# Cross-attention with layer norm: a tile's scores with 128 rows as weights in place of 64

## The chip, the cores and the metric

The kernel runs on one NeuronCore of a Trainium2 chip. The metric is device time in microseconds (us) of one execution. Three runs of the kernel before took 506.99 to 508.13 us, median 507.49.

The engines are called as in the profile: PE is TensorE, and its matmuls; PEld is TensorE's loading of weights, the operand that stays in the array while the other one streams past; DVE is VectorE, ACT is ScalarE, POOL is GpSimd, SP issues transfers (DMA).

## The reference

Four sequences of 2048 rows of 512 numbers attend to 77 context rows each, with 16 heads of 32 numbers. Then comes an output projection, the residual and a layer norm. All is fp32.

```python
qs = (q @ wq).reshape(Bq, Lq, H, HD).transpose(0, 2, 1, 3)       # H = 16, HD = 32
ks_ = (k @ wk).reshape(Bq, Lk, H, HD).transpose(0, 2, 1, 3)      # Lk = 77
vs = (v @ wv).reshape(Bq, Lk, H, HD).transpose(0, 2, 1, 3)
scores = jnp.einsum('bhqd,bhkd->bhqk', qs, ks_) / jnp.sqrt(jnp.float32(HD))
scores = jnp.where(mask[:, None, :, :], -jnp.inf, scores)
attn_w = jax.nn.softmax(scores, axis=-1)
attn = jnp.einsum('bhqk,bhkd->bhqd', attn_w, vs)
attn = attn.transpose(0, 2, 1, 3).reshape(Bq, Lq, H * HD)
out = attn @ wo + q
mu = jnp.mean(out, axis=-1, keepdims=True)
var = jnp.mean((out - mu) ** 2, axis=-1, keepdims=True)
return (out - mu) / jnp.sqrt(var + EPS) * gamma + beta
```

## The kernel before

The 8192 rows are 64 tiles of 128 rows. Keys and values are made once, at the start. Then each tile goes through these steps, each of them a word in a long table, `ORDER`, that is written out by hand and read from left to right; every engine works off its own instructions in that order.

- `Q`: the queries of four tiles, kept transposed: 512 rows of x stream past the weights `wq`. A product of high precision is made of three fp32r matmuls, of rounded parts (`q_rows`, line 275). VectorE copies the result to `q` (line 289).
- `S`: the scores of a tile (line 405), the step that is changed.
- `T`: VectorE adds the mask to the scores and takes each row's maximum (line 422); it reads them from the bank that TensorE wrote.
- `e`, `r`, `n`: exponentials by ScalarE (line 437), reciprocals by VectorE, the product by GpSimd (line 452).
- `t`, `P`: VectorE transposes 32x32 blocks (line 473), and transfers regroup them (line 484).
- `V`: the weights times the values, of two tiles at once (line 498), split into two parts for the next step by ScalarE and VectorE.
- `O`: the output projection (line 554), again three matmuls for each product. Residual, moments, scale, gain, shift and store follow on the other engines.

So TensorE's queue is a sequence of visits: 12 matmuls for a fourth of a `Q`, 12 for an `O`, a visit for the values, a visit for the scores. Between words, 62 visits make the scores of 64 tiles: 60 of one tile, and two, early in the run, of two tiles.

In `scores`, the queries of the tile are the weights and the keys stream. A head has 32 numbers, so it uses a band of 32 of the array's 128 rows, and the four heads j of a group lie on the four bands. `SR` is how many rows of the tile one matmul takes as weights, which are as many columns of the array. With 64, the two halves r0 = 0 and 64 of a tile use the left and the right half of the columns, and their results go to the lower and the upper 64 partitions of the bank. A group has so eight matmuls on eight pieces of the array, and a tile has four groups. Each fp32 matmul of the program runs as two pairs of a weight load and a matmul.

```python
SR = 64                                                        # line 42
...
for g in range(NG):                                            # line 401, four groups
    for r0 in range(0, P, SR):
        for j in range(GH):                                    # four heads of a group
            q = slice(HD * j, HD * (j + 1))
            mm = nc.tensor.matmul(
                sc[j][r0 : r0 + SR, g * NK : (g + 1) * NK],    # line 406, out
                qs[q, g, rs.start + r0 : rs.start + r0 + SR],  # weights: 32 x SR
                kct[q, g, t // TPB, keys_of(j)],               # streams: 32 x 77
                start=True,
                stop=True,
            )
```

Of the kernel before, what the change touches and what calls it, by code (L numbers as in the profile page):

```python
# [38 lines left out]
MASKED = -3.38e38  # L39
EPS = 1.0e-5  # L40
WARM = 9
SR = 64
NPB = 3
KSCALE = 1.0 / HD**0.5
LAST = 56
# [129 lines left out]
def xattn_layernorm(  # L175
# [74 lines left out]
    def keys_of(h):  # L250
        return slice(TAIL_K, NK2) if h % 2 == 0 else slice(0, NK)
# [145 lines left out]
    def scores(t):  # L397
# [3 lines left out]
        for g in range(NG):  # L401
            for r0 in range(0, P, SR):
                for j in range(GH):
                    q = slice(HD * j, HD * (j + 1))
                    mm = nc.tensor.matmul(  # L405
                        sc[j][r0 : r0 + SR, g * NK : (g + 1) * NK],
                        qs[q, g, rs.start + r0 : rs.start + r0 + SR],
                        kct[q, g, t // TPB, keys_of(j)],
# [392 lines left out]
```

## Time and profile before

| what | us |
|---|---|
| median of three runs | 507.49 |
| span of the profiled execution | 506.2 |
| PE busy | 498.8 |
| ACT busy | 473.9 |
| DVE busy | 460.5 |
| POOL busy | 421.3 |
| scores' matmuls (line 405), busy | 61.2 |
| scores' weight loads (line 405), busy | 51.4 |

The profile is of one execution. The page gives its span, from the first to the last instruction, and no time of its own beyond that. Busy times count a moment once however many instructions of a kind run in it, so many small matmuls side by side show a busy time far below the sum of their lengths. In a row of the timeline the first number is the start, the second the length of the whole group of equal instructions that follow each other, and "x64" their count; a row is cut to what falls in the stretch that was asked for. A shape such as 32*64 behind a matmul is the piece of the array in rows and columns.

### The profile page before, as it was taken

The numbers are of one execution on the slowest core, as the hardware profiler recorded it, in microseconds if no ns is written. First come the engines' busy times: TensorE is split into PE (matmuls) and PEld (weight loads), VectorE is DVE, ScalarE is ACT, GpSimd is POOL, SyncE is SP. The second block draws the span as 40 slices with busy tenths as digits, with TensorE's granted clock in tenths as the row PEclk, the third lists the DMA queues.
The fourth block names the chain that finished last, engine by engine and source line by source line (L and its number), as shares of the span: only waits on it lengthen the run. The fifth ranks groups of instructions, "written<-read, shape, count | busy, mean of one in ns | idle before, by whom it ended". The sixth has DMA issues, their size and how long they took to land.

```text
span 506.2 us, 20312 instructions
## 1 busy us (share of the span) xinstructions
PE 498.8 (99%) x6831; PEld 383.1 (76%) x6831; DVE 460.5 (91%) x2539; ACT 473.9 (94%) x2248; POOL 421.3 (83%) x387
## 2 busy tenths in 40 slices
PE   9999999999999999999999999999999999999995
PEld 6987778777777777777777777777777777877773
DVE  5799988999899999898898898998999999899997
ACT  6699999999999999999999999999999998999851
POOL 2666464789886798989989887999998999999896
PEclk9999999999999999999999999999999999999999
DMA  8957577889886796859887778877888769888746
GB/s 306 396 197 175 135 212 183 221 210 217 247 242 178 177 248 199 249 165 253 243 216 204 200 207 240 230 201 193 248 232 225 207 177 293 247 199 222 183 150 232
DMA packets 58782, 110.86 MB, mean 219 GB/s; under 512 B 9462, under 2 KB 11278, under 8 KB 58678
## 3 DMA queue, kind: packets, MB, share of 16 engines
q1 hardware_dynamic: 54502, 101.30, 71.1%
q0 software_dynamic: 2496, 5.77, 4.0%
q10 hardware_dynamic: 1680, 2.49, 2.0%
q8 instruction: 54, 0.88, 0.8%
q14 instruction: 50, 0.41, 0.3%
HBM read 41.79 MB, written 16.78 MB: 116 GB/s over the span
## 4 chain that ended last, share of the span: by engine, by line
PE 98%; DMA 1%; DVE 1%; ACT 0%; issue 0%; DVEq 0%
PE po L554 36%; PE pq L275 35%; PE pa L498 11%; PE sc L405 11%; PE pv L326 2%; PE pk L299 1%; PE pq L685 1%; DMA stage_a<-kin 1%; PE pa L513 0%; DVE xtl L637 0%; PE po L543 0%; DVE st L606 0%; DVE po L634 0%; ACT woh L672 0%; DVE mvt L608 0%
## 5 line engine op out<-in xcount | busy, mean ns | idle before, releaser
L437 ACT ACTIVATE pbuf<-pbuf,nm 128x77 f32<-128x77 f32 x1024 | 353.0, 358 | 5.2 <-DVE nm L422 3.6
L437 ACT ACTIVATION_READ_ACCUMULATOR pbuf<-pbuf,nm 128x1 f32 x1024 | 203.2, 198 | 0.0
L422 DVE CUSTOM_DVE_ANT_0 pbuf<-sc,mb 128x77 f32<-128x77 f32 x1024 | 169.7, 231 | 7.4 <-PE sc L405 5.8
L452 POOL TENSOR_TENSOR pbuf<-pbuf,ri 128x1232 f32<-128x1232 f32 x63 | 142.2, 2258 | 36.7 <-DVE ri L447 25.4
L554 PE MATMUL po<-woh,AH 128*128 128x512 f32 x256 | 103.5, 404 | 0.0
L473 DVE STREAM_TRANSPOSE B<-pbuf 128x1280 f32<-128x1280 f32 x64 | 96.1, 1502 | 5.8 <-POOL pbuf L452 2.4
L275 PE MATMUL pq<-xth,wqh 128*128 128x512 f32 (+1 forms) x256 | 100.8, 394 | 0.2
L554 PE MATMUL po<-wol,AH 128*128 128x512 f32 x256 | 99.9, 390 | 0.0
L554 PE MATMUL po<-woh,AL 128*128 128x512 f32 x256 | 99.8, 390 | 0.0
L275 PE MATMUL pq<-xth,wql 128*128 128x512 f32 (+1 forms) x256 | 98.1, 383 | 0.0
L275 PE MATMUL pq<-xtl,wqh 128*128 128x512 f32 (+1 forms) x256 | 98.1, 383 | 0.0
L422 DVE DVE_READ_ACCUMULATOR2_ANT nm<- 128x1 f32 x1024 | 84.4, 82 | 0.0
L598 POOL TENSOR_TENSOR o<-o,bet 128x512 f32<-128x512 f32 x56 | 72.1, 1291 | 1.8
L595 POOL TENSOR_TENSOR o<-o,gam 128x512 f32<-128x512 f32 x56 | 72.2, 1293 | 0.1
L269 POOL TENSOR_TENSOR xtl<-xtf,xth 128x1024 fp32r<-128x1024 f32 x28 | 67.2, 2404 | 3.9 <-ACT xth L265 3.2
L405 PEld LDWEIGHTS sc<-kct,q 32*64 32x64 f32 x4096 | 51.4, 130 | 22.6 <-issue 12.2
L405 PE MATMUL sc<-kct,q 32*64 32x77 f32 x4096 | 61.2, 238 | 0.0
L498 PE MATMUL pa<-PT,vsb 96*32 96x256 f32 x992 | 59.7, 382 | 0.0
L554 PEld LDWEIGHTS po<-woh,AH 128*128 128x128 f32 x256 | 48.0, 188 | 14.3 <-issue 2.5
L275 PEld LDWEIGHTS pq<-xth,wqh 128*128 128x128 f32 x256 | 48.1, 188 | 13.7 <-DVE nm L422 1.2
L554 PEld LDWEIGHTS po<-woh,AL 128*128 128x128 f32 x256 | 48.1, 188 | 10.5 <-DVE AL L531 0.2
L275 PEld LDWEIGHTS pq<-xth,wql 128*128 128x128 f32 x256 | 48.1, 188 | 9.7
(108 smaller groups left out, 638.6 us busy)
## 6 DMA issues: line engine op xcount, KB each, us to landing
PT<-B SPq DMA_DIRECT2D x330, 128.0 KB
xtf<-xT SPq DMA_DIRECT2D x28, 512.0 KB
o<-x SPq DMA_DIRECT2D x56, 256.0 KB
out<-o SPq DMA_DIRECT2D x56, 256.0 KB
PT<-B POOLq DMA_DIRECT2D x25, 128.0 KB, 4.0
PT<-B ACTq DMA_DIRECT2D x17, 128.0 KB
stage_a<-kin SPq DMA_DIRECT2D x4, 410.0 KB
xtf<-xT SPq DMA_DIRECT2D x4, 256.0 KB
```

Of the source, the lines that this page charges most:

```text
L269: return nc.gpsimd.tensor_tensor(l[:, c : c + 2], fx.pop((g, c)), xh[g][:, c : c + 2].bitcast(F32), ALU.subtract)
L275: nc.tensor.matmul(pq, w[:, c, m * P : (m + 1) * P], r[g][:, c, rs], start=(n == 0), stop=(n == 11))
L326: nc.tensor.matmul(pv[: rows.stop - rows.start], ctx_s[c][i][:, rows], v[c], start=(n == 0), stop=(n == 11))
L405: mm = nc.tensor.matmul(sc[j][r0 : r0 + SR, g * NK : (g + 1) * NK], qs[q, g, rs.start + r0 : rs.start + r0 + SR], kct[q, g, t // TPB, keys ...
L422: nc.vector.tensor_tensor_reduce(pb[:, h // 2, (h % 2) * NK : (h % 2 + 1) * NK], scs[t][j][:, g * NK : (g + 1) * NK], mb[:, t % TPB, keys_ ...
L437: nc.scalar.activation(pb[:, h // 2, (h % 2) * NK : (h % 2 + 1) * NK], pb[:, h // 2, (h % 2) * NK : (h % 2 + 1) * NK], AF.Exp, bias=nmax[t ...
L452: return nc.gpsimd.tensor_tensor(pv, pv, rv.to_broadcast((P, NP, 2, NK)), ALU.mult)
L473: nc.vector.transpose(bt.rearrange("p c q r -> p q c r"), pbuf[t % NPB].rearrange("p q (c r) -> p q c r", c=5),)
L498: nc.tensor.matmul(pas[b, g // 2][HD * j : HD * (j + 1), (g % 2) * BLK : (g % 2 + 1) * BLK], vsb[:, 2 * b // TPB, h % 2, HD * (h // 2) : H ...
L554: nc.tensor.matmul(pos[t], a[:, c, rs], w[:, c, :], start=(first and c == 0 and n == 0), stop=(c == NC_D - 1 and n == 2),)
L595: return nc.gpsimd.tensor_tensor(od[t], od[t], gam, ALU.mult)
L598: return nc.gpsimd.tensor_tensor(od[t], od[t], bet, ALU.add)
```

## The change

`SR` becomes 128. The loop over r0 then has one step, so a group has four matmuls in place of eight, each with all 128 rows of the tile as weights: 32 rows by 128 columns of the array. A tile has 16 matmuls in the program in place of 32, which run as 32 pairs of a load and a matmul in place of 64.

```diff
-SR = 64
+SR = 128
```

On PE, around a visit for the scores late in the program, this stood before (`sc_0` to `sc_3` are the banks of the four heads j, `64x77` is what the matmul writes):

```order
L275 MATMUL pq_2_8052<-xth_7130,wql 128x512
L405 MATMUL sc_0_8065<-kct,q_7425 64x77
L405 MATMUL sc_1_8066<-kct,q_7425 64x77
L405 MATMUL sc_2_8067<-kct,q_7425 64x77
L405 MATMUL sc_3_8068<-kct,q_7425 64x77
L405 MATMUL sc_0_8065<-kct,q_7425 64x77
```

And the same place now:

```order
L275 MATMUL pq_2_7108<-xth_6298,wql 128x512
L405 MATMUL sc_0_7121<-kct,q_6561 128x77
L405 MATMUL sc_1_7122<-kct,q_6561 128x77
L405 MATMUL sc_2_7123<-kct,q_6561 128x77
L405 MATMUL sc_3_7124<-kct,q_6561 128x77
L405 MATMUL sc_0_7121<-kct,q_6561 128x77
```

Before, the second row of `sc_0` is the other half of the same group; now it is the next group. Only the numbers behind the names differ otherwise: on PE all else stands where it stood, between the same neighbours, and on the other engines every instruction does.

## Prediction

> **What bounds the kernel now.** I read the page's busy shares first, then the chain of work that ended last, then two stretches of the run by themselves.
>
> ```profile
> span 506.2 us, 20312 instructions
> PE 498.8 (99%) x6831; PEld 383.1 (76%) x6831; DVE 460.5 (91%) x2539; ACT 473.9 (94%) x2248; POOL 421.3 (83%) x387
> PE 98%; DMA 1%; DVE 1%; ACT 0%; issue 0%; DVEq 0%
> 58.50:204.00 145.50, 145.50 (x2067) 111.65 (x2067) 134.97 (x793) 145.06 (x710) 111.80 (x92) 1.00 0.79 211
> 204.00:465.50 261.50, 261.49 (x3797) 198.69 (x3796) 241.18 (x1391) 256.80 (x1239) 241.91 (x216) 1.00 0.81 222
> ```
>
> The third line is the chain: TensorE alone makes 98% of it. In the two stretches (columns: length; busy PE, PEld, DVE, ACT, POOL; clock) PE has no gap at all, at the full granted clock of 1.00. ScalarE is the next, with 0.44 us free in the first stretch and 4.7 us in the second. So whatever a visit of TensorE to the scores costs more or less is first paid by TensorE's own queue. The other engines matter only if TensorE gets faster. The scores' two groups on the page:
>
> ```profile
> L405 PEld LDWEIGHTS sc<-kct,q 32*64 32x64 f32 x4096 | 51.4, 130 | 22.6 <-issue 12.2 <-DVE nm L422 5.1 <-DVE q L289 1.6
> L405 PE MATMUL sc<-kct,q 32*64 32x77 f32 x4096 | 61.2, 238 | 0.0
> ```
>
> 4096 over 64 tiles is 64 loads and 64 matmuls for a tile, twice the 32 that the program writes: each fp32 matmul runs as two load-and-matmul pairs. 32*64 is the piece of the array that one uses, 32 rows by 64 columns, so eight fit side by side: four bands of rows (the four heads of a group), two halves of the columns (the two halves of the tile).
>
> **One visit, before.** The timeline of PE around two visits (start, length, count):
>
> ```profile
> 204.41 0.39 PE L275 MATMUL pq<-xth,wql 128*128 128x512 f32 x1
> 204.72 0.95 PE L405 MATMUL sc<-kct,q 32*64 32x77 f32 x64
> 205.61 1.93 PE L498 MATMUL pa<-PT,vsb 96*32 96x256 f32 x32
> ...
> 207.47 0.95 PE L405 MATMUL sc<-kct,q 32*64 32x77 f32 x64
> 208.35 0.50 PE L554 MATMUL po<-woh,AH 128*128 128x512 f32 x1
> 208.69 0.39 PE L554 MATMUL po<-wol,AH 128*128 128x512 f32 x1
> 208.93 0.39 PE L554 MATMUL po<-woh,AL 128*128 128x512 f32 x1
> 209.15 0.39 PE L554 MATMUL po<-woh,AH 128*128 128x512 f32 x1
> ```
>
> From the first matmul of a visit to the first of the next work it is 0.89 us (204.72 to 205.61) and 0.88 us (207.47 to 208.35): take 0.885. Its last matmul starts 0.95 - 0.225 = 0.725 us after its first (0.225 is the usual length of one, from the listing of this line below), so 0.16 us lie between that last start and the next work.
>
> ```profile
> L405 PEld LDWEIGHTS sc<-kct,q x64: 127/131/132, 204.7 to 205.4; 32*64 32x64 f32 x64
> L405 PE MATMUL sc<-kct,q x64: 224/225/276, 204.7 to 205.5; 32*64 32x77 f32 x64
> 204.72 0.17 PEld L405 LDWEIGHTS sc<-kct,q 32*64 32x64 f32 x8 [0.35 <-DVE B L473]
> 204.78 0.24 PEld L405 LDWEIGHTS sc<-kct,q 32*64 32x64 f32 x16
> 204.84 0.24 PEld L405 LDWEIGHTS sc<-kct,q 32*64 32x64 f32 x16
> 204.91 0.20 PEld L405 LDWEIGHTS sc<-kct,q 32*64 32x64 f32 x9
> ```
>
> The last four rows are looks at the loads at four moments, each showing the start of the oldest load still running. Eight loads start within 0.055 us, about 0.007 apart, one for each piece of the array. The next eight begin at 204.78, then 204.84 and 204.91: a first round of 0.06, then rounds of 0.06 to 0.07. A piece has room for one load ahead: each round begins when the matmuls of the one before do. Eight rounds (four groups, two pairs each) at 0.067 would put the last start at about 0.06 + 7 x 0.067 + 0.05 = 0.58 us; it is at 0.725, so the visit also loses some 0.15 us in its later part. The changed visit has half the instructions and should not lose that, which is in its favour.
>
> **The change, part by part.** Removed: half of the pairs, 32 of 64 loads and 32 of 64 matmuls for a tile. Added: each load that stays brings 128 columns in place of 64. The matmuls that stay stream the same 77 columns of keys. Four pieces of the array work side by side in place of eight, so there are still eight rounds, one after the other on each band of rows. What a round costs is therefore the larger of two things: the matmul, which the rounds above bound at 0.067, and the load of 128 columns. Its price stands in other places of the same trace:
>
> ```profile
> 208.35 0.19 PEld L554 LDWEIGHTS po<-woh,AH 128*128 128x128 f32 x1
> 208.46 0.19 PEld L554 LDWEIGHTS po<-wol,AH 128*128 128x128 f32 x1
> 208.70 0.19 PEld L554 LDWEIGHTS po<-woh,AL 128*128 128x128 f32 x1
> ...
> 22.65 0.19 PEld L275 LDWEIGHTS pq<-xth,wqh 128*128 128x128 f32 x1 [0.19 <-PE sc L405]
> 22.75 0.19 PEld L275 LDWEIGHTS pq<-xtl,wqh 128*128 128x128 f32 x1
> 22.87 0.19 PEld L275 LDWEIGHTS pq<-xth,wql 128*128 128x128 f32 x1
> 22.99 0.19 PEld L275 LDWEIGHTS pq<-xth,wqh 128*128 128x128 f32 x1
> 23.11 0.19 PEld L275 LDWEIGHTS pq<-xtl,wqh 128*128 128x128 f32 x1
> ```
>
> After a pause nothing else delays the first load, and the second begins once it is in: 0.11 us later at 208.35 and 0.10 at 22.65, against 0.06 for 64 columns above. That is the lower bound, 0.10. The upper one is 0.12, the step of the 256-column matmuls from 22.75 on; but 256 columns at the 512-column step (208.93 to 209.15, 0.22 to 0.23 us) already take 0.11 to 0.115, so those rows may be held by the matmul and not by the load. I take 0.11, from the pair at 208.35, where nothing but the load is timed. It is well over the matmul's 0.067, so the load becomes the bound of the round.
>
> A visit then: eight loads one after the other on a band, 0.88, plus 0.02 for the fourth band's later start (three steps of 0.007), plus the same 0.16 to the next work: 1.06 us. Against 0.885 that is +0.17. With 0.10 it is 0.98 (+0.095), with 0.12 it is 1.14 (+0.255).
>
> Not all visits are single. Early in the run two visits take two tiles each:
>
> ```profile
> 20.86 1.76 PE L405 MATMUL sc<-kct,q 32*64 32x77 f32 x128
> 28.46 1.76 PE L405 MATMUL sc<-kct,q 32*64 32x77 f32 x128
> ```
>
> Such a visit costs 1.76 - 0.225 + 0.16 = 1.70 before and 16 x 0.11 + 0.02 + 0.16 = 1.94 after: +0.24. So 60 x 0.17 + 2 x 0.24 = 10.7 us. From this I take 0.2 for short waits of TensorE on other engines, which a later arrival shortens: +10.5 us. By the bounds, 0.10 gives 60 x 0.095 + 2 x 0.08 = 5.9, and 0.12 gives 60 x 0.255 + 2 x 0.40 = 16.1.
>
> The rest costs nothing. The order of the program is the same on every engine. A bank of scores is finished 0.17 us later within a visit, and VectorE, which waits for it, has 7% to 8% free in the two stretches. ScalarE behind it gains slack, since TensorE sets the pace. No transfer of data is added or moved.
>
> One rule speaks for a far dearer change. The Trainium skill, "TensorE: Matmul & The Clock Gate", section "Part 3: Packing small matmuls — row/col tiling", says that weight loads overlap running matmuls only when these use other row groups. By it load and matmul would add up on each band, and the visit would be the third rival below. The trace disagrees for this kernel: the load at 208.70 begins while a matmul from 208.69 to 209.08 holds all 128 rows.
>
> **The sum.** The profiled execution has a span of 506.2 us; the median of the three timed runs is 507.49, 1.3 us more, which I take as what lies around the span. Span 516.7, time 507.5 + 10.5 = 518.0 us.
>
> **Rivals.** First, *a faster kernel: the longer load is hidden*. If a load of 128 columns into 32 rows took no longer than one of 64, a round stayed at 0.067 and the visit cost 0.06 + 7 x 0.067 + 0.02 + 0.16 = 0.71 us: -0.175 each, -11 us for TensorE. For it: eight loads ran side by side above, so loads share no single path. Against it: those eight went to eight different pieces, and 0.11 against 0.06 is what twice the columns cost elsewhere. The balance is where 8 rounds + 0.18 make 0.885, a round of 0.088; below that the kernel is faster. ScalarE caps this gain: it has only 0.44 + 4.7 = 5.1 us free between 58.5 and 465.5, so the time would be about 502.5. The same page of the Trainium skill, section "Weight-path perf modes — Fast Weight Load (FWL) and DoubleRow", puts a faster load on when there are 128 weight columns, but not for FP32, so by that rule this rival does not come true here. Chance 7%.
>
> Second, *no change: the switch costs less*. The last L275 matmul above starts at 204.41 and would let the next in at 204.64 (0.23 later); the scores start at 204.72, and after their last matmul another 0.09 of the 0.16 is more than its round. If pieces that use all columns, as the neighbours do, needed no such pause on either side, the visit would win back 0.17, just what the loads cost: about 507.5. Against it: the pause stands at every kind of switch shown, also into the 96*32 work at 205.61. Chance 5%.
>
> Third, *slower by far: load and matmul add up*, 8 x (0.11 + 0.067) + 0.18 = 1.60 us for a visit, +0.71 x 64 = 45: about 553 us. Against it the overlap at 208.70, and the rounds of 0.067 above, which hold a load of 0.06 and a matmul at once. Chance 3%.
>
> **How the numbers follow.** My forecast has 85%: 518.0 us, by its bounds 513.4 to 523.6. Only cases worth 15% lie outside these, so the range is nearly its own, widened to 512.5 and 524.5 for what the rounding of rows to 0.01 us leaves open. About 0.2% (1 us) is what a measurement of this kernel can tell from no change. Faster: the first rival and a little of the second, 0.08. Same: the rest of the second, 0.05. Slower: 0.87.
>
> **What would show it.** In the changed profile the scores' groups should count 2048 each with pieces of 32*128, loads near 190 ns, and 32 matmuls in a single visit, which lasts about 1.06 us to the next work. Loads of one band should start 0.11 apart, with the pauses around the visit as before, and the chain should give the scores' line 13% in place of 11%, TensorE still at 98%. The forecast is wrong if a round is near 0.07 (first rival) or 0.18 (third), if the pauses of 0.09 are gone (second), or if visits are longer as said and the span does not follow.

## The result and the profile after

The changed kernel takes 519.57 us (median of 4 runs, 519.08 to 520.27), against 507.25 us (median of 4). The ratio is 1.0231 with a 95% interval of 1.0207 to 1.0255, so it is slower by 10.5 to 12.9 us. The profiled execution has a span of 517.4 us and took 519.26 us. The span of before was 506.2, so the span grew by 11.2.

The page after, its span, busy shares and chain by engine and by line:

```profile
span 517.4 us, 16136 instructions
PE 510.2 (99%) x4783; PEld 395.2 (76%) x4783; DVE 460.8 (89%) x2539; ACT 475.2 (92%) x2248; POOL 421.7 (82%) x387
...
PE 94%; ACT 2%; DVE 2%; DMA 1%; ACTq 0%; issue 0%; SPq 0%; DVEq 0%
PE po L554 33%; PE pq L275 33%; PE sc L405 12%; PE pa L498 10%; PE pv L326 2%; PE pk L299 1%; ACT pbuf L437 1%; PE pq L685 1%; DMA stage_a<-kin 1%; DVE pbuf L422 1%; DMA PT<-B 1%; PE pa L513 0%; DVE xtl L637 0%; DVE B L473 0%; ACTq L484 0%; PE po L543 0%
```

TensorE is busy 11.4 us longer. VectorE, ScalarE and GpSimd are busy as long as before, within 1.3 us. The two groups of the scores, by the listing of groups:

```profile
L405 PEld LDWEIGHTS sc<-kct,q 32*128 32x128 f32 x2048 | 62.9, 186 | 22.6 <-issue 10.1
L405 PE MATMUL sc<-kct,q 32*128 32x77 f32 x2048 | 72.1, 277 | 0.0
```

Half as many loads and matmuls as before, on pieces of 32*128, and yet TensorE spends 72.1 us in them in place of 61.2: +10.9 of the 11.2 us lie in this one line.

The same two visits as before, on PE's timeline (start, length, count):

```profile
208.96 0.39 PE L275 MATMUL pq<-xth,wql 128*128 128x512 f32 x1
209.28 1.13 PE L405 MATMUL sc<-kct,q 32*128 32x77 f32 x32
210.34 1.93 PE L498 MATMUL pa<-PT,vsb 96*32 96x256 f32 x32
212.21 1.13 PE L405 MATMUL sc<-kct,q 32*128 32x77 f32 x32
213.27 0.50 PE L554 MATMUL po<-woh,AH 128*128 128x512 f32 x1
```

A visit takes 1.06 us to the next work (209.28 to 210.34, 212.21 to 213.27), where it was 0.885. The pause ahead of it is the same: 208.96 + 0.23 = 209.19, and the scores start at 209.28. Its loads on the timeline, seen at five moments (each row starts with the oldest load still running), and behind them the listing of line 405 for this visit (shortest, median and longest in ns, first and last start in us):

```profile
209.28 0.20 PEld L405 LDWEIGHTS sc<-kct,q 32*128 32x128 f32 x4 [0.35 <-DVE B L473]
209.39 0.20 PEld L405 LDWEIGHTS sc<-kct,q 32*128 32x128 f32 x4
209.50 0.21 PEld L405 LDWEIGHTS sc<-kct,q 32*128 32x128 f32 x4
209.61 0.21 PEld L405 LDWEIGHTS sc<-kct,q 32*128 32x128 f32 x4
209.72 0.21 PEld L405 LDWEIGHTS sc<-kct,q 32*128 32x128 f32 x4
```

```profile
L405 PEld LDWEIGHTS sc<-kct,q x32: 181/187/187, 209.3 to 210.1; 32*128 32x128 f32 x32
L405 PE MATMUL sc<-kct,q x32: 270/270/329, 209.3 to 210.1; 32*128 32x77 f32 x32
```

Four loads start together, one on each band, and the next four 0.11 us later, every time. Before, the rounds were 0.06 to 0.07.

### The profile page after: what moved, and what is told of

It reads as the page before. It is cut to its first block, busy times and chain, and to the rows that moved or that the text cites. A ratio compares the mean times of both kernels' runs of the same rounds, so it can differ in the third digit from the quotient of the medians.

```text
span 517.4 us, 16136 instructions
## 1 busy us (share of the span) xinstructions
PE 510.2 (99%) x4783; PEld 395.2 (76%) x4783; DVE 460.8 (89%) x2539; ACT 475.2 (92%) x2248; POOL 421.7 (82%) x387
## 4 chain that ended last, share of the span: by engine, by line
PE 94%; ACT 2%; DVE 2%; DMA 1%; ACTq 0%; issue 0%; SPq 0%; DVEq 0%
PE po L554 33%; PE pq L275 33%; PE sc L405 12%; PE pa L498 10%; PE pv L326 2%; PE pk L299 1%; ACT pbuf L437 1%; PE pq L685 1%; DMA stage_a<-kin 1%; DVE pbuf L422 1%; DMA PT<-B 1%; PE pa L513 0%; DVE xtl L637 0%; DVE B L473 0%; ACTq L484 0%; PE po L543 0%
## 5 line engine op out<-in xcount | busy, mean ns | idle before, releaser
L437 ACT ACTIVATION_READ_ACCUMULATOR pbuf<-pbuf,nm 128x1 f32 x1024 | 197.9, 193 | 0.0
L405 PEld LDWEIGHTS sc<-kct,q 32*128 32x128 f32 x2048 | 62.9, 186 | 22.6 <-issue 10.1
L598 POOL TENSOR_TENSOR o<-o,bet 128x512 f32<-128x512 f32 x56 | 72.1, 1290 | 1.8
L405 PE MATMUL sc<-kct,q 32*128 32x77 f32 x2048 | 72.1, 277 | 0.0
```

The costliest lines, as they stand in the source:

```text
L405: mm = nc.tensor.matmul(sc[j][r0 : r0 + SR, g * NK : (g + 1) * NK], qs[q, g, rs.start + r0 : rs.start + r0 + SR], kct[q, g, t // TPB, keys ...
L437: nc.scalar.activation(pb[:, h // 2, (h % 2) * NK : (h % 2 + 1) * NK], pb[:, h // 2, (h % 2) * NK : (h % 2 + 1) * NK], AF.Exp, bias=nmax[t ...
L598: return nc.gpsimd.tensor_tensor(od[t], od[t], bet, ALU.add)
```

## The experiments

The theory: a round on a band is the larger of its matmul and its weight load. Before, it was the matmul of 77 columns at 0.067 us; now it is the load of 128 columns at 0.11. Two things about it could be otherwise. The round might be longer because of the matmul, which has twice the results to write. And the visit before lost some 0.15 us in its later part, which the prediction put down to half the instructions without showing it.

### More columns streamed, with 64 weight columns

Each scores matmul streams 128 columns of keys in place of 77. The 51 more are other keys, and their results are not read.

```diff
-                        sc[j][r0 : r0 + SR, g * NK : (g + 1) * NK],
+                        sc[j][r0 : r0 + SR, g * P : (g + 1) * P],
                         qs[q, g, rs.start + r0 : rs.start + r0 + SR],
-                        kct[q, g, t // TPB, keys_of(j)],
+                        keys[q, g, k0(t) + keys_of(j).start : k0(t) + keys_of(j).start + P],
...
-                scs[t][j][:, g * NK : (g + 1) * NK],
+                scs[t][j][:, g * P + off(t) : g * P + off(t) + NK],
```

> The kernel before (64 weight columns), but each scores matmul streams 128 key columns in place of 77; the 51 more are other keys, and what they give is not read. Theory (a round is the larger of its matmul and its load; before, the matmul of 77 columns at 0.067 us was the larger): a round becomes about 0.109, as long as the changed kernel's 0.112, and the visit about 1.06 us to the next work in place of 0.88: +0.18 on each of 64, about +11.5 us, some 519 us. The 0.15 us that a visit lost in its later part should vanish, since slower rounds leave time for it; if it stays, the visit is 1.21 and the time 528. Rival (rounds are set by the count of pairs that are issued, not by what they stream): no change, 507.

It took 523.4 us against 508.49 us of the kernel before in the same comparison, a ratio of 1.0284 (1.0251 to 1.0318); the span is 521.8. A visit on its timeline, and behind it the listing of the line (412 here) for this visit:

```profile
211.02 1.21 PE L412 MATMUL sc<-kct,q 32*64 32x128 f32 x64
212.16 0.64 PE L505 MATMUL pa<-PT,vsb 96*32 96x256 f32 x8
```

```profile
L412 PEld LDWEIGHTS sc<-kct,q x64: 127/131/132, 211.0 to 211.9; 32*64 32x64 f32 x64
L412 PE MATMUL sc<-kct,q x64: 266/268/319, 211.0 to 212.0; 32*64 32x128 f32 x64
```

The visit is 1.14 us (211.02 to 212.16), neither 1.06 nor 1.21. The same loads (131 ns) with a longer stream make it longer, so with 64 weight columns the stream does set the pace, and the rival that only counts pairs falls. But of the 0.15 us in the later part about half remains: the last matmul starts 1.21 - 0.27 = 0.94 us after the first, and eight rounds of 0.109 alone would put it at 0.06 + 7 x 0.109 + 0.05 = 0.87.

### More columns streamed, with 128 weight columns

The same edit on the changed kernel (SR = 128).

> The changed kernel (128 weight columns), with 128 key columns streamed in place of 77; the 51 more are not read. Theory (the load of 128 columns sets the round at 0.112): a matmul of 128 columns at about 0.109 still lies beneath it, so rounds stay at 0.112. Only the last matmul of a visit is longer, by 0.043 us: +2.7 us over the changed kernel, span about 520, time about 522. Rival (the round is set by the matmul, for instance because a matmul over 128 weight columns has twice the results to write): rounds grow by 128/77 to 0.186, the visit by 0.6 us, the time by 38 us to about 557.

521.27 us, ratio 1.0242 (1.0202 to 1.0282) to before; span 519.8, 2.4 us over the changed kernel's. Its loads at four moments on the timeline of PEld, and behind them a visit on that of PE:

```profile
210.25 0.20 PEld L412 LDWEIGHTS sc<-kct,q 32*128 32x128 f32 x4 [0.35 <-DVE B L480]
210.36 0.20 PEld L412 LDWEIGHTS sc<-kct,q 32*128 32x128 f32 x4
210.47 0.21 PEld L412 LDWEIGHTS sc<-kct,q 32*128 32x128 f32 x4
210.58 0.21 PEld L412 LDWEIGHTS sc<-kct,q 32*128 32x128 f32 x4
```

```profile
210.25 1.17 PE L412 MATMUL sc<-kct,q 32*128 32x128 f32 x32
211.35 1.93 PE L505 MATMUL pa<-PT,vsb 96*32 96x256 f32 x32
```

The rounds are still 0.11, with 66% more columns streamed. The visit is 1.10 us, longer by 0.04, the last matmul's own growth. This is what the theory said, and the rival (557 us) is out: even the matmul of 128 streamed columns, whose rounds are 0.109 us apart in the trace of the run above, still fits under the load. A cost of the matmul that was the same for 77 and for 128 columns would look alike here. Against it stands the load's own price: on a piece that was idle, the second load starts 0.028, 0.055 and 0.109 us after the first with 32, 64 and 128 weight columns (traces of the run with 32 below, of before and of after), so the load of 128 columns alone fills the round.

So on the same 51 columns more, the kernel with 64 weight columns loses 0.26 us a visit and the one with 128 loses 0.04. That is the difference between a round bound by the stream and one bound by the load.

### 32 weight columns

```diff
-SR = 64
+SR = 32
```

> SR = 32: 64 matmuls in the program for a tile, 128 pairs, on sixteen pieces of 32 rows by 32 columns. Loads of 32 columns take 0.028 us, matmuls stay at 0.067, so by the array alone a visit would be 0.03 + 7 x 0.067 + 0.1 + 0.16 = 0.76 us: -0.12, about 500 us. Theory (the later part of a visit before is set by how fast new instructions come to TensorE's queue, about 16 of the program's matmuls in some 0.3 us after a pause of 0.06): the first 16 start at once, the other 48 come one after the other at about 0.017 us from 0.38 us on, so the last starts near 1.25 and the visit takes about 1.4 us: +0.52, +33 us, about 540. Between the two means that the queue limits less than I think.

597.57 us, ratio 1.174 (1.168 to 1.180). A visit that nothing else held, and one of the others, on PE's timeline:

```profile
208.38 1.56 PE L405 MATMUL sc<-kct,q 32*32 32x77 f32 x128
209.88 1.93 PE L498 MATMUL pa<-PT,vsb 96*32 96x256 f32 x32
...
244.98 1.40 PE L405 MATMUL sc<-kct,q 32*32 32x77 f32 x109
249.47 0.38 PE L405 MATMUL sc<-kct,q 32*32 32x77 f32 x19 [3.10 <-issue]
249.78 0.50 PE L554 MATMUL po<-woh,AH 128*128 128x512 f32 x1
```

The first is 1.50 us long, near the 1.4 expected and twice the 0.76 that the array alone would need. The start of such a visit, first in the kernel before and then here, cut where 32 pairs (16 of the program's matmuls) have started:

```profile
204.72 0.52 PE L405 MATMUL sc<-kct,q 32*64 32x77 f32 x32
208.38 0.42 PE L405 MATMUL sc<-kct,q 32*32 32x77 f32 x32
```

Before, these 32 start within 0.52 - 0.225 = 0.30 us, at the pace of the rounds, and the other 32 need until 0.73, 0.43 us more, where four rounds of 0.067 would take 0.27. Here the first 32 start within 0.19 us, and the other 96 need until 1.56 - 0.225 = 1.34, that is 0.38 us for each 32. So from the 17th of the program's matmuls on both visits go at nearly the same pace, on pieces of different size, and the array alone would be faster in both. This is where the 0.15 us of the visit before are lost: in its second half. That it is the pace at which instructions reach the array is inferred from this; it was not seen directly.

The time was missed by 58 us. In the second visit TensorE stands still for 3.10 us, and the timeline names nothing that it waits for. By the listing of waits there are several such:

```profile
PE sc L405 <- issue: 24.2, 12, 4.4
PE pa L498 <- issue: 6.3, 5, 2.6
```

The columns are the total, the times and the longest. None of this size stands in the profile of before, where the longest of TensorE's waits of that name is 0.7 us. What arrives late can be read from the pages' tables of DMA queues (packets, MB, share), here of before, of after and of this run:

```profile
q8 instruction: 54, 0.88, 0.8%
q8 instruction: 38, 0.62, 0.5%
q8 instruction: 86, 1.41, 1.1%
```

The 16 packets fewer and the 32 more are 64 bytes for each load or matmul fewer or more (4096 and 8192), so this queue brings TensorE its instructions, 256 in a packet of 16384 bytes. In the trace each of the 17 waits of the listing ends 1.2 to 1.6 us after the end of such a packet; the one that ends at 249.47 follows a packet from 246.70 to 248.17. By this timing TensorE has run out of instructions there and waits for the next packet. Why these packets come too late was not tested.

The waits make 30.5 of the 89.2 us by which the span is longer than before. The granted clock adds to it: about the end of each of the six longest, of 2.4 to 4.4 us, it falls to 0.5 for 3.4 or 6.8 us. This is a stretch behind the wait that ends at 249.47 (columns as in the prediction, the clock third from the end):

```profile
250.40:253.60 3.20, 3.20 (x9) 2.55 (x8) 2.25 (x29) 3.20 (x19) 2.07 (x1) 0.50 0.73 209
```

The work between the visits takes 13 us more, its waits not counted, most of it in such stretches. What is left, some 46 us, is the visits themselves, for which 33 were expected.

### 32 weight columns for one tile in four

```diff
+            sr = 32 if t % 4 == 1 else SR
-            for r0 in range(0, P, SR):
+            for r0 in range(0, P, sr):
```

> SR = 32 for one tile in four (t = 1, 5, 9, ...), the other 48 as before. With SR = 32 everywhere a visit that nothing else held took 1.34 us to its last matmul's start and 0.155 on (1.49, +0.61 over 0.88), but 36 of 62 visits were longer, by 32 us in all, with waits of TensorE that end with nothing the profile shows. Theory A (those waits come when too many instructions are asked for over a long stretch: 28503 in place of 20312): a quarter of the added instructions leaves them out, so 16 x 0.61 = +9.8 us, about 518. Theory B (every visit of 64 matmuls brings its own share of such waits): +0.5 us more for each, +18 us, about 526.

530.97 us (528.54 and 533.39) against 507.49 us, ratio 1.046 (1.035 to 1.058); the span of the faster run is 526.8, 20.6 us over that of before. In size this is nearer to B (18 us) than to A (9.8). But the waits are not spread over the visits, as B had it. There are few, such as the 3.03 us here:

```profile
467.08 1.51 PE L406 MATMUL sc<-kct,q 32*32 32x77 f32 x123
471.62 0.33 PE L406 MATMUL sc<-kct,q 32*32 32x77 f32 x5 [3.03 <-issue]
471.88 0.50 PE L555 MATMUL po<-woh,AH 128*128 128x512 f32 x1
```

while another visit of 64 matmuls shows none:

```profile
105.20 1.56 PE L406 MATMUL sc<-kct,q 32*32 32x77 f32 x128
106.70 0.64 PE L499 MATMUL pa<-PT,vsb 96*32 96x256 f32 x8
```

The listing has three ahead of scores matmuls, and two of 0.8 and 0.4 us ahead of other work:

```profile
PE sc L406 <- issue: 5.7, 3, 3.0
```

Two of the three, those that end at 32.85 and 401.21, stand in visits that have 64 weight columns. So neither theory holds as it was put: a wait falls wherever a packet of instructions is late, and all five end 1.2 to 1.4 us after one, as above. They are 6.9 of the 10.8 us beyond A; the rest was not traced.

### The change on the odd tiles alone

```diff
-            for r0 in range(0, P, SR):
+            for r0 in range(0, P, SR << t % 2):
```

with `SR << t % 2` in the two slices too.

> The change on the odd tiles alone: 32 tiles with 128 weight columns, 32 with 64. Theory (all of the cost lies in the visit itself, on TensorE's queue): half of it, +5.6 in the span and about +6 us, 513, with visits of 0.88 and of 1.06 side by side. Rival (part of the 12.3 us is a shift of the whole schedule against ScalarE or VectorE, which a smaller delay would not set off): less than half, under +4 us.

513.2 us, ratio 1.0086 (1.0053 to 1.0120) to 508.49, that is 2.7 to 6.1 us; span 511.3, 5.1 us over that of before.

```profile
206.70 1.13 PE L405 MATMUL sc<-kct,q 32*128 32x77 f32 x32
207.76 1.93 PE L498 MATMUL pa<-PT,vsb 96*32 96x256 f32 x32
209.63 0.95 PE L405 MATMUL sc<-kct,q 32*64 32x77 f32 x64
210.51 0.50 PE L554 MATMUL po<-woh,AH 128*128 128x512 f32 x1
```

A visit of 1.06 us and one of 0.88, side by side, each as it is in its own kernel. The listing of groups, by shape:

```profile
L405 PE MATMUL sc<-kct,q 32*128 32x77 f32 x1024 | 36.2, 277 | 0.0
L405 PE MATMUL sc<-kct,q 32*64 32x77 f32 x2048 | 30.6, 237 | 0.0
```

TensorE is 66.8 us in the scores, 5.6 more than the 61.2 of before, half of the 10.9. So the cost lies in the visits, one by one: from first matmul to next work, the 62 visits take 5.1 us more than before, as much as the span. That is a little under half of the 11.2 us. The interval of the timed runs alone would still allow the rival's under 4 us.

## Why the prediction was right

The forecast was 518.0 us, +10.5; measured were 519.57 and +12.3 (10.5 to 12.9).

- *What bounds the kernel.* Right: TensorE's busy time grew by 11.4 us and the span by 11.2.
- *The load of 128 columns at 0.11 us.* Right: the rounds are 0.11 (209.28, 209.39, 209.50, 209.61, 209.72). The price came from a pair of loads after a pause in quite other work, with 128 rows in place of 32. That the load sets the round and not the matmul is shown by the two runs with 128 columns streamed: no change of the round with 128 weight columns, +0.26 us a visit with 64.
- *The visit.* 1.06 us predicted and measured. The two visits with two tiles, predicted at 1.94, are 2.02 - 0.27 + 0.20 = 1.95:

```profile
21.07 2.02 PE L405 MATMUL sc<-kct,q 32*128 32x77 f32 x64
28.83 2.02 PE L405 MATMUL sc<-kct,q 32*128 32x77 f32 x64
```

  Within the visit two parts were off against each other. The last matmul starts at 1.13 - 0.27 = 0.86 and not 0.90, and 0.20 lie behind it and not 0.16. A matmul is shown 270 ns long in place of 225, so it seems to be shown as started while its load still runs; the sum is the same.

  The two visits with two tiles took longer before than the prediction had worked out, 1.82 and 1.86 us to the next work and not 1.70. They start at 20.86 and 28.46, and these follow:

```profile
22.68 0.36 PE L275 MATMUL pq<-xth,wqh 128*128 128x256 f32 x1
...
30.32 0.47 PE L275 MATMUL pq<-xth,wqh 128*128 128x512 f32 x1
```

  So they cost 0.25 us more together and not 0.48. The 60 single visits cost 0.18 each and not 0.17, 0.5 us more in all. These two misses are of opposite sign, and that they partly cancel is luck.
- *The 0.15 us lost in the later part before.* Right that the changed visit does not lose it. The run with 32 columns gives a reason: from the 17th of the program's matmuls on, a visit goes at some 0.4 us for 16 of them, with 32 columns as with 64. The changed visit has just 16, and its rounds stay at 0.11 to the end.
- *0.2 us taken off for short waits.* Of this next to nothing came. Before, nine of the single visits took longer than 0.89 us, by 0.6 us in all (the one at 255.08 took 1.08); why is not shown. After, a single one does, with a new wait of TensorE in front of the output projection at 412.51:

```profile
410.90 1.34 PE L405 MATMUL sc<-kct,q 32*128 32x77 f32 x32
412.51 0.50 PE L554 MATMUL po<-woh,AH 128*128 128x512 f32 x1 [0.27 <-DVE AL L531]
```

  This visit takes 1.61 us to the next work in place of 1.06, which is nearly all that the nine gave back. In sum the 62 visits take 68.1 us in place of 57.2, which is 10.9 of the 11.2 us of the span. The chain leaves TensorE at this wait, and this is why it shows 94% and not the 98% that I named as a sign, and 12% for the scores' line and not 13%.
- *The time around the span.* I took 1.3 us, the median of three runs less the span of one execution, whose own time I did not have. Wherever both are on record for one run they are 1.7 to 1.9 us apart, for the kernel before (508.21 and 506.4) as for the changed one (519.26 and 517.4). So of the 1.6 us by which the forecast was low, 0.5 lie here and 0.7 in the span (517.4 in place of 516.7). The 12.3 us hold some spread of their own: the kernel before had medians of 507.25 to 508.49 in three comparisons.
- *The rivals.* Rounds are neither near 0.07 nor near 0.18, and the pause of 0.09 ahead of the visit stands, so all three are out. The load does overlap the matmul on its own band: a round of 0.11 holds both, where the sum would be 0.177. That again disagrees with the overlap rule that the prediction names from the Trainium skill, "TensorE: Matmul & The Clock Gate", section "Part 3: Packing small matmuls — row/col tiling".

No experiment beat the kernel before.

## What to carry to other kernels

Many small matmuls side by side had three prices here: the stream on each piece of the array, the weight load on each piece, and the pace at which instructions arrive. Work out each one for a round before choosing the size: the best of 32, 64 and 128 weight columns was the middle one, where the load (0.06 us) just fits under the stream (0.067). Fewer and larger instructions are no gain where the load grows past the stream, and the price of that load could be read ahead of the change from the first two loads after a pause elsewhere in the trace.

## What the runs showed of the hardware that was not expected

- The first 16 of the program's fp32 matmuls of a visit (32 pairs of load and matmul) start within 0.30 us with 64 columns and within 0.19 with 32. Those behind them need 0.43 and 0.38 us for 16.
- TensorE's instructions come over a DMA queue of their own, 64 bytes each and 256 in a packet. With 28503 instructions in place of 20312 TensorE runs out of them 17 times, for up to 4.4 us and 30.5 us in all, and each wait ends 1.2 to 1.6 us after a packet has landed.
- About the end of each of the six longest of these waits (2.4 us and more) the granted clock fell to 0.5 for 3.4 or 6.8 us; behind the others it did not.
- With 128 weight columns and 77 streamed a matmul is shown 45 ns longer than with 64 (270 against 225). It is no fixed addition: with 128 streamed the two are shown with 270 and 268.
